# An fp32 sum of 64 features, as two products of 32 features on the column quarters of the PE array

## The chip, the cores and the metric

The kernel runs on one core of a Trainium2 chip. A core has five engines: TensorE (PE, matrix products, with its weight loads shown apart as PEld), VectorE (DVE), ScalarE (ACT), GpSimd (POOL) and SyncE (SP), which issues most DMAs. The metric is the time of one execution on the device in microseconds, the median of several runs. The profile is of one further execution; its span is from the first to the last instruction.

## What is computed

Four graph layers over 3,327 nodes with 64 features, all with the same dense-stored adjacency matrix `adj` (3,327 x 3,327, fp32). Each begins with a layer norm and a ReLU and adds to `x`. What costs time is the product with `adj`, or with a matrix made of it, eight times in a row:

```python
# layer 0: two gated cells            (k = 0, 1)
m = adj @ (h @ W);  ... sigmoid, tanh ...
# layer 1: ranked neighbours          (k = 2)
mask = (adj != 0);  rank = cumsum(mask, axis=1)
w = mask * where(pos > 0, 0.5 ** (k - pos), 0)
out = w @ (h @ weight) + bias
# layer 2: squared weights            (k = 3, 4, 5)
w = adj * adj
for W, b in ((W0, b0), (W1, b1), (W2, b2)):
    x = (w @ x) @ W.T + b
# layer 3: two hops                   (k = 6, 7)
agg = adj @ x;  x = tanh(concatenate([agg, x], 1) @ W[k])
```

## The kernel before

**Tiling.** The nodes are padded to 3,328 and cut into two halves of 13 blocks of 128. The host lays `adj` out transposed. A source block (`Tile`, number `q`, 26 of them) brings 128 source nodes on the partitions and, for each half `h` of the targets, a range of target columns. The 13 target blocks of a half are cut into four chunks, `CH`, of 384, 384, 384 and 512 columns, held in two groups (`GROUPS`). The last sum cuts its second chunk once more, into 256 and 128 columns (`PARTS`).

**A step.** `propagate(k, c, t, ...)` (L579) adds source block `t` to sum `k` of chunk `c`. The stationary operand is the 128 x 64 block of features `yq` of the source nodes, the moving one the 128 x w block of `adj`. It does so once for each target half: half 0 writes to PSUM partitions 0 to 63 of the chunk's accumulator, half 1 to partitions 64 to 127. So the first product sits on the left 64 columns of the PE array, the second on the right 64. These are L605 to L608:

```python
for n, yq in enumerate(terms):
    for h in range(2):
        nc.tensor.matmul(acc[h][1][h * D:(h + 1) * D, :w], yq[h], rhs[h], ...)
```

In seven of the eight sums (`KIND` is PLAIN or SQUARED) both operands are fp32 and there is one term. In the ranked sum (`KIND[2]` is RANKED) both are bf16 and there are three terms a step. 7 sums x 26 sources x 4 chunks, and 26 more for the last sum's extra part, make 754 fp32 steps.

**What stands between the steps.** One order of PE instructions is made when the program is built. `joint` (L655) and `alone` list the steps: sum k of a group of chunks, with steps of sum k + 1 put in between once their sources are known. `run` walks the list. It puts in:
- `count` (L533, products on L542, bf16, 64 columns for each half): the number of non-zero entries of each target column, four products for a source block. They come after nearly every pair of steps of the sums k = 0 and 1.
- `expand` (L484): for the ranked sum the mask is multiplied by a triangular matrix `tri` (through `mm`, L307, bf16, 64 columns), and ACT (L523) or DVE (L521) turns the ranks into powers of two.
- after a chunk's last step, a task `after_k`: copies out of PSUM (L824 on ACT, L825 on DVE), the gates (L876), transposes and small weight products on PE (L307, L774, L791), layer norm (L834 to L849), which makes the features of the next sum.

A task is advanced by `spend`, which takes an estimate of PE time for each step. The order of every engine is thereby fixed at build time; semaphores only hold an instruction back. All products of the kernel before use column tiles of 64.

**Buffers.** 20 slots of SBUF hold source blocks; SP loads them (L405) up to 44 steps ahead. PSUM has eight banks, four for sums and four for temporaries.

Of the kernel before, what the change touches and what calls it, by code (L numbers as in the profile page):

```python
# [44 lines left out]
N, D = 3327, 64  # L45
# [25 lines left out]
PLAIN, RANKED, SQUARED = range(3)  # L71
KIND = [PLAIN, PLAIN, RANKED, SQUARED, SQUARED, SQUARED, PLAIN, PLAIN]
# [11 lines left out]
def chunk_of(b):  # L84
    return next(c for c, (b0, b1) in enumerate(CH[:NC]) if b0 <= b < b1)
# [11 lines left out]
def kernel(  # L97
# [9 lines left out]
    nc = tc.nc  # L107
# [191 lines left out]
    def width(c):  # L299
        return blocks(c) * P  # L300
# [15 lines left out]
    def take(sums=False, either=True):  # L316


        either = either and not sums
        pool = idle_sums if sums else idle_temps  # L320
        if either and idle_sums and (not pool or released[idle_sums[0]] < released[pool[0]]):
            pool = idle_sums
        for c in list(tasks):
            if not pool and c not in running:
                advance(c)
        i = pool.popleft()
        return i, banks[i]
# [25 lines left out]
    def advance(c):  # L353
        running.add(c)
        try:
            tasks[c][1] = next(tasks[c][0])
        except StopIteration:
            del tasks[c]
        running.discard(c)

    def begin(c, task):
        finish(c)
        tasks[c] = [task, 0.0]
        advance(c)

    def finish(c):
        while c in tasks:
            advance(c)
# [5 lines left out]
    def spend(us):  # L374

        for c in list(tasks):
            if c in tasks and c not in running:
                tasks[c][1] -= us
                if tasks[c][1] <= 0:
                    advance(c)  # L380
# [79 lines left out]
    def make_mask(t, kind):  # L460

        t.mask = Mask(t.w)
        rows = P - 1 if kind == RANKED else P

        def piece(half):
            nc.vector.tensor_scalar(t.mask.view[:rows, half], t.view()[:rows, half], 0.0, None, op0=ALU.not_equal)  # L466
            if half == 0 and kind == RANKED:

                for ch in GROUPS[t.g]:
                    finish(("count", ch))  # L470
                nc.gpsimd.dma_start(out=t.mask.view[P - 1:P], in_=totals[t.g][t.q:t.q + D + 1:D, :])  # L471
            if half == 1:
                t.used()

        pieces.extend([(t, 0, piece), (t, 1, piece)])
# [57 lines left out]
    def count(t, first, last):  # L533


        mask_pieces(t=t)
        for c in GROUPS[t.g]:
            w = width(c)
            if first:
                counts[c] = take(either=False)  # L540
            for s in range(2):
                nc.tensor.matmul(counts[c][1][s * D:(s + 1) * D, :w], behind[:, NQ - 1 - t.q:NQ - 1 - t.q + D],  # L542
                                 t.mask.view[:, s, t.cols(c)], start=first, stop=last)
            spend(STREAM_US * w / CWM * 0.25)
            if last:
                begin(("count", c), count_done(c))
        t.mask.free()
# [31 lines left out]
    def propagate(k, c, t, rhs, first, last):  # L579
        if k == COUNT:  # L580
            count(t, first, last)
            return
        w = width(c)
        if first:
            sums[k, c] = [take(sums=True) for _ in range(2 if k == 7 and c == PARTS[1] else 1)]
            sums[k, c] = [sums[k, c][0], sums[k, c][-1]]
        acc = sums[k, c]
        if t is SPECIAL:
            for ch in range(NC):
                while y[k][ch] is None:  # L590
                    advance(ch)
            terms = [[lasty[:, h, i, :] for h in range(2)] for i in range(3)]
            rhs = [rhs, rhs]
        else:
            s, b = divmod(t.q, NB)
            cs = chunk_of(b)
            if y[k][cs] is None:
                finish(cs)
            terms = [[yk[:, b - CH[cs][0], s, :]] * 2 for yk in (y[k][cs] if KIND[k] == RANKED else [y[k][cs]])]
            rhs = [rhs[:, h, :] for h in range(2)]  # L600
            if KIND[k] != RANKED:
                t.used()
            if (k, c, t) in squared:
                squared.pop((k, c, t)).free()
        for n, yq in enumerate(terms):  # L605
            for h in range(2):
                nc.tensor.matmul(acc[h][1][h * D:(h + 1) * D, :w], yq[h], rhs[h], start=first and n == 0,  # L607
                                 stop=last and n == len(terms) - 1)  # L608
        if t is not SPECIAL and t.early and t.mask is None:
            make_mask(t, RANKED)  # L610
        spend(STREAM_US * w / CWM * (0.75 if KIND[k] == RANKED else 1.0))
        if last:
            begin(c, after[k](c, sums.pop((k, c))))
# [97 lines left out]
    def run():  # L711
# [5 lines left out]
        for i, (k, c, t) in enumerate(units):  # L717
# [24 lines left out]
            elif all(y[2][ch] is not None for ch in GROUPS[0]):  # L742
                relief["pieces"] = t is not SPECIAL
                if i % 2 == 0:
                    mask_pieces(1)
            n = done[k, c] = done.get((k, c), 0) + 1
            propagate(k, c, t, expanded.popleft(), n == 1, n == total[k, c])


# [336 lines left out]
```

## Time and profile before

| | us |
|---|---|
| median of 3 runs | 706.8 (706.53 to 707.41) |
| span of the profiled execution | 703.7 |
| DVE and ACT busy | 350.1 and 271.8 |
| longest single wait of PE after the start | 0.9 |
| DMA: mean rate over the span | 286 GB/s |

The profiled execution's span is 3.1 us less than the median of the runs, which include what lies around the instructions.

How to read the views. "Busy" of an engine is the time in which at least one of its instructions is under way. A matmul's end is modelled and includes the time that the pipeline takes to empty, so a busy PE may still have room; what counts is the distance between the starts of passes. In a group, "128*64" is rows times columns of the PE array, "128x384" the moving operand; "xN" the number of instructions, then the busy time, the mean duration in ns, and the idle time ahead of them with what ended it. In the chain of waits each piece has its start and its length in us. The slices are tenths of 40 equal parts of the span.

The waits of PE, longest first in total, with times and longest single wait:

```profile
PE temp L791 <- DVE y L849: 14.9, 1, 14.9
PE sum L307 <- DVE e L521: 1.4, 2, 0.9
PE temp L542 <- DVE adj L466: 0.7, 2, 0.5
PE sum L607 <- DVE y L849: 0.6, 1, 0.6
```

The first is the wait for the first features; the others together are some 4 us.

Busy time of the engines in four stages: to 137 us and from there to 205 us (the first two sums, with their counts between them), to 345 us (the ranked sum beside fp32 sums, from the first instruction of L523 at 204.5 us on), and the rest, nearly all fp32. The numbers in brackets are instructions; the last three columns are the granted clock, the busy share of the DMA engines and GB/s:

```profile
0.00:137.00 137.00, 121.19 (x859) 74.27 (x861) 84.06 (x168) 17.33 (x31) 15.03 (x32) 1.00 0.86 332
137.00:205.00 68.00, 67.78 (x494) 31.99 (x491) 42.59 (x86) 14.61 (x26) 18.05 (x25) 1.00 0.81 291
205.00:345.00 140.00, 136.71 (x1374) 98.90 (x1372) 110.42 (x213) 113.87 (x199) 39.68 (x53) 1.00 0.63 218
345.00:704.00 359.00, 354.11 (x2382) 167.78 (x2378) 113.04 (x282) 125.97 (x169) 7.24 (x5) 1.00 0.78 294
```

### The profile page before, as it was taken

To read this page: it belongs to the slowest core of one execution; us is meant where nothing else is said; L and a number is where in the kernel's file an instruction comes from. 1 tells how busy PE (TensorE), PEld (TensorE's weight loads), DVE (VectorE), ACT (ScalarE), POOL (GpSimd) and SP (SyncE) were. 2 spreads that over 40 slices of the span, in tenths; PEclk is the share of its full clock that TensorE was granted. 3 is DMA by queue.
4 is the path that set the end of the run, shared out by engine and by line. 5 is a ranking of instruction groups with operands and counts; after the bars stand their busy time and mean duration, and the time that the engine had idled before them with its cause. 6 is when DMAs were issued, how large, how long until landed. Compare 5 with 4: busy or idle time off the path is not lost.

```text
span 703.7 us, 12628 instructions
## 1 busy us (share of the span) xinstructions
PE 679.8 (97%) x5100; PEld 372.9 (53%) x5100; DVE 350.1 (50%) x746; ACT 271.8 (39%) x422; POOL 80.0 (11%) x114
## 2 busy tenths in 40 slices
PE   1999999999999999999999999999999999999997
PEld 1454666643556787677444444333344444344586
DVE  7556835643997889847523105425271565005101
ACT  1014100122146888888998206832166600000101
POOL 4300000002284233111100000000000000000000
PEclk9999999999999999999999999999999999999999
DMA  9999996089686952683799649973998399927991
GB/s 344 401 385 404 406 405 241 2 314 398 209 279 253 371 177 76 246 297 96 265 390 343 245 151 409 405 276 100 398 366 271 107 391 406 406 81 276 402 403 45
DMA packets 68549, 201.31 MB, mean 286 GB/s; under 512 B 7228, under 2 KB 8228, under 8 KB 68492
## 3 DMA queue, kind: packets, MB, share of 16 engines
q1 hardware_dynamic: 65596, 199.46, 75.9%
q8 instruction: 40, 0.66, 0.4%
q10 hardware_dynamic: 720, 0.85, 0.3%
q0 software_dynamic: 2176, 0.20, 0.2%
q14 instruction: 17, 0.14, 0.1%
HBM read 199.45 MB, written 0.85 MB: 285 GB/s over the span
## 4 chain that ended last, share of the span: by engine, by line
PE 91%; DVE 7%; issue 0%; ACT 0%; DMA 0%; POOL 0%; ACTq 0%; DVEq 0%; POOLq 0%
PE sum L607 77%; PE temp L307 5%; PE temp L542 2%; PE temp L876 2%; PE sum L307 1%; DVE adj L466 1%; PE temp L774 1%; PE sum L876 1%; DVE e L521 1%; DVE st L842 1%; DVE adj L901 1%; DVE t L836 1%; DVE y L841 0%; DVE st L834 0%; DMA xs<-in_x 0%
## 5 line engine op out<-in xcount | busy, mean ns | idle before, releaser
L607 PE MATMUL sum<-adj,y 128*64 128x384 f32 (+3 forms) x3016 | 534.5, 502 | 0.7 <-DVE y L849 0.6
L607 PEld LDWEIGHTS sum<-adj,y 128*64 128x64 f32 x3016 | 243.5, 137 | 237.3 <-issue 212.4
L440 ACT ACTIVATE adj<-adj 128x768 f32<-128x768 f32 (+1 forms) x176 | 144.2, 893 | 45.8 <-PE sum L607 21.9
L466 DVE TENSOR_SCALAR adj<-adj 128x768 bf16<-128x768 f32 (+3 forms) x208 | 114.0, 597 | 39.8 <-PE temp L542 31.8
L824 ACT COPY both<-sum 64x384 f32<-64x384 f32 (+3 forms) x17 | 8.1, 478 | 192.6 <-PE sum L607 191.4
L607 PE MATMUL sum<-e,both 128*64 128x384 bf16 (+1 forms) x624 | 78.5, 339 | 0.5 <-DVE e L521 0.5
L523 ACT ACTIVATE e<-temp,bitsb 128x384 int16<-128x384 f32 (+1 forms) x117 | 66.0, 605 | 15.1 <-PE temp L307 9.9
L825 DVE COPY both<-sum 64x384 f32<-64x384 f32 (+3 forms) x17 | 9.6, 569 | 110.5 <-ACT both L824 110.5
L307 PE MATMUL temp<-adj,tri 128*64 128x384 bf16 (+1 forms) x332 | 56.8, 341 | 0.5 <-DVE e L521 0.2
L442 DVE TENSOR_TENSOR adj<-adj 128x768 f32<-128x768 f32 (+1 forms) x32 | 30.6, 1005 | 52.1 <-DMA adj<-in_adjT 33.4
L845 POOL TENSOR_TENSOR st<-st,mhalf 128x6 f32<-128x6 f32 (+1 forms) x16 | 24.0, 1498 | 283.2 <-DVE st L843 279.5
L607 PEld LDWEIGHTS <-both 128*64 128x64 bf16 x624 | 46.6, 110 | 15.5 <-issue 2.2
L307 PEld LDWEIGHTS <-tri 128*64 128x64 bf16 x416 | 33.5, 110 | 15.3 <-issue 7.1
L521 DVE TENSOR_SCALAR e<-temp 128x384 int16<-128x384 f32 (+1 forms) x49 | 30.1, 617 | 21.1 <-ACT e L523 10.5
L471 POOL DMA_DIRECT2D adj<-totals x52 | 31.5, 607 | 51.2 <-PE temp L307 40.9
L803 DVE STREAM_TRANSPOSE both<-y 32x96 f32<-32x96 f32 (+1 forms) x128 | 35.6, 278 | 2.9
L542 PE MATMUL temp<-adj,behind 128*64 128x384 bf16 x208 | 30.3, 339 | 0.9 <-DVE adj L466 0.7
L819 DVE STREAM_TRANSPOSE y<-t 32x96 f32<-32x96 f32 (+1 forms) x64 | 17.8, 278 | 24.9 <-ACT t L810 24.0
L542 PEld LDWEIGHTS <-behind 128*64 128x64 bf16 x208 | 17.0, 110 | 17.6 <-issue 15.9
L755 DVE COPY t<-sum 128x384 f32<-128x384 f32 x6 | 3.3, 555 | 35.3 <-PE sum L607 35.3
L564 POOL MEMSET adj<- 128x768 f32 (+1 forms) x2 | 1.9, 950 | 145.3 <-PE sum L607 145.3
L523 ACT ACTIVATE e<-sum,bitsb 128x384 int16<-128x384 f32 (+1 forms) x28 | 16.6, 598 | 2.5 <-PE sum L307 2.1
(132 smaller groups left out, 327.8 us busy)
## 6 DMA issues: line engine op xcount, KB each, us to landing
adj<-in_adjT SPq DMA_DIRECT2D x130, 768.0 KB, 8.5
adj<-in_adjT SPq DMA_DIRECT2D x104, 896.0 KB, 12.3
xs<-in_x SPq DMA_DIRECT2D x1, 640.0 KB
adj<-totals POOLq DMA_DIRECT2D x26, 3.0 KB, 5.1
adj<-totals POOLq DMA_DIRECT2D x26, 3.5 KB, 3.0
out<-xs ACTq DMA_DIRECT2D x2, 192.0 KB
out<-xs ACTq DMA_DIRECT2D x1, 256.0 KB
stage<-in_weights SPq DMA_DIRECT2D x2, 112.0 KB, 13.1
```

Of the source, the lines that this page charges most:

```text
L307: nc.tensor.matmul(out[hs], lhsT[:, hs], rhs, start=start, stop=stop)
L440: nc.scalar.activation(sq, v, AF.Square)
L442: nc.vector.tensor_tensor(sq, v, v, ALU.mult)
L466: nc.vector.tensor_scalar(t.mask.view[:rows, half], t.view()[:rows, half], 0.0, None, op0=ALU.not_equal)
L471: nc.gpsimd.dma_start(out=t.mask.view[P - 1:P], in_=totals[t.g][t.q:t.q + D + 1:D, :])
L521: nc.vector.tensor_scalar(wide[:, s], ps[:, :w], BITS, 0.0, op0=ALU.add, op1=ALU.max)
L523: nc.scalar.activation(wide[:, s], ps[:, :w], AF.Relu, bias=bitsb)
L542: nc.tensor.matmul(counts[c][1][s * D:(s + 1) * D, :w], behind[:, NQ - 1 - t.q:NQ - 1 - t.q + D], t.mask.view[:, s, t.cols(c)], start=firs ...
L607: nc.tensor.matmul(acc[h][1][h * D:(h + 1) * D, :w], yq[h], rhs[h], start=first and n == 0, stop=last and n == len(terms) - 1)
L803: nc.vector.transpose(to[at:at + 32, :, q], h[q * 32:(q + 1) * 32, :, s, f * 32:(f + 1) * 32])
L845: nc.gpsimd.tensor_tensor(st[:, 3, :n], st[:, 2, :n], mhalf[:, :n], ALU.pow)
L876: nc.tensor.matmul(ps[upper(1 - s), :w], cells[:, cell, s, g, :], both[c][:, s], start=True, stop=True)
```

## The change

Every fp32 step now issues four products instead of two. The 64 features of the stationary operand are cut into two runs of 32. For each run `f` and each target half `h`, a product of 32 columns is put at PSUM partitions h x 64 + f x 32, with its place in the array given as `tile_position=(0, at)`: the array works as four column tiles of 32. The moving operand of a half is read by two products, f = 0 and f = 1. The order is quarter 0, 64, 32, 96. The steps of the ranked sum, the counts, the masks' products and all small products stay as they were, on two column tiles of 64.

```diff
-        for n, yq in enumerate(terms):
-            for h in range(2):
-                nc.tensor.matmul(acc[h][1][h * D:(h + 1) * D, :w], yq[h], rhs[h], start=first and n == 0,
-                                 stop=last and n == len(terms) - 1)
+        if KIND[k] != RANKED:
+            for f in range(2):
+                for h in range(2):
+                    at = h * D + f * 32
+                    nc.tensor.matmul(acc[h][1][at:at + 32, :w], terms[0][h][:, f * 32:(f + 1) * 32], rhs[h],
+                                     start=first, stop=last, tile_position=(0, at))
+        else:
+            for n, yq in enumerate(terms):
+                for h in range(2):
+                    nc.tensor.matmul(acc[h][1][h * D:(h + 1) * D, :w], yq[h], rhs[h], start=first and n == 0,
+                                     stop=last and n == len(terms) - 1)
```

Line numbers after this place are seven higher in the changed kernel; the fp32 products are its L609, the ranked ones L614. Nothing else is changed: the estimates that `spend` takes, the list of steps and the order of the other engines are the same.

## The prediction

> **What bounds the kernel now.** I read the page's engine shares and slices first, then the chain of waits, then the groups of PE by shape, then single stretches in the timeline.
>
> The page, its span, engine shares, slices, chain and two groups:
>
> ```profile
> span 703.7 us, 12628 instructions
> PE 679.8 (97%) x5100; PEld 372.9 (53%) x5100; DVE 350.1 (50%) x746; ACT 271.8 (39%) x422; POOL 80.0 (11%) x114
> ...
> PE   1999999999999999999999999999999999999997
> ...
> PEclk9999999999999999999999999999999999999999
> ...
> PE 91%; DVE 7%; issue 0%; ACT 0%; DMA 0%; POOL 0%; ACTq 0%; DVEq 0%; POOLq 0%
> ...
> L607 PE MATMUL sum<-adj,y 128*64 128x384 f32 (+3 forms) x3016 | 534.5, 502 | 0.7 <-DVE y L849 0.6
> L607 PEld LDWEIGHTS sum<-adj,y 128*64 128x64 f32 x3016 | 243.5, 137 | 237.3 <-issue 212.4
> ```
>
> PE is busy from 15 us to the end at the full granted clock, and the changed line is 534.5 us of it, with 0.7 us of idle time before it. The fp32 products of L607 are 1,508 in the program (754 steps of one source block and one chunk, two halves each), yet 3,016 stand in the profile: an fp32 product runs as two passes, each with its own weight load.
>
> How full is the array? The chain of waits has long stretches that hold nothing else:
>
> ```profile
> 365.98 41.28 PE sum L607 x256
> ...
> 413.73 90.87 PE sum L607 x504
> ```
>
> The first is all 384 columns wide: 41.28 us / 256 = 161 ns a pass. A step has four passes, so 645 ns, although one pass lasts 486 ns in the trace. So the two halves stream beside each other, each pass taking 322.5 ns of its half. By the clock that the Trainium skill gives (2.4 GHz; TensorE: Matmul & The Clock Gate, its table of specifications) 384 columns x 4 cycles are 640 ns. The measured 645 leaves 5 ns a step, about 4 us over 754 steps: the columns are all in use, and there is nothing for quarters to fill in such a stretch. Over the whole kernel, 7 sums x 26 sources x 1,664 columns = 302,848 columns of each half, at 645/384 = 1.68 ns, make 509 us.
>
> Two more facts from the timeline and the groups by shape:
>
> ```profile
> 68.51 0.76 PE L876 MATMUL temp<-both,cells 128*64 128x384 f32 x2
> 68.84 0.49 PE L542 MATMUL temp<-adj,behind 128*64 128x384 bf16 x2
> 69.11 0.49 PE L876 MATMUL temp<-both,cells 128*64 128x384 f32 x1
> 69.16 0.60 PE L542 MATMUL temp<-adj,behind 128*64 128x384 bf16 x2
> ```
>
> In the program all passes of this L876 gate stand ahead of the L542 counts, yet two counts start before the last gate pass. The halves take their work independently: the upper half runs ahead while the lower one is still behind. The second fact is the price of a fresh start, from the groups by shape in 341.2 to 341.5 us (after a wait) and in 420.0 to 420.3 us (in a full stream):
>
> ```profile
> L607 PE MATMUL sum<-adj,y 128*64 128x384 f32 x2 | 0.5, 537 | 0.6 <-DVE y L849 0.6
> ```
> ```profile
> L607 PE MATMUL sum<-adj,y 128*64 128x384 f32 x4 | 0.8, 486 | 0.0
> ```
>
> A pass whose weights were not loaded ahead lasts 51 ns more (537 against 486). And 486 against 322.5 says that 164 ns of a pass are the pipeline emptying behind it, hidden as long as the next pass follows.
>
> **What the Trainium skill says.** TensorEngine Tiling (Array Packing), Key Properties: "Mode switching requires drain: Changing tiling mode (not just tile) drains the TensorE". Before has only 64-column tiles, so its trace shows no switch and neither confirms nor denies it. The same section says that tiles operate independently; the timeline above agrees. TensorE: Matmul & The Clock Gate, Part 3, Measured speedup, gives 2.38 times for three column tiles of 32, so quarters do run beside each other; no run here shows a quarter. The same part has matmuls in strict FIFO; the lines at 68.8 us contradict that across halves, and the measurement decides.
>
> **The change part by part.**
>
> Removed and added: every fp32 step (L607, kinds other than RANKED) had two products of 64 columns and gets four of 32, so 1,508 products become 3,016, and 3,016 passes become 6,032, each as wide as before (128 to 512 columns of the moving operand). No instruction of DVE, ACT, POOL or SP is added or moved; the order of these engines and of the DMAs is the same. All bf16 products (L307, L542, the ranked L607) and the small fp32 ones (L774, L791, L876) keep 64-column tiles.
>
> Streaming: a quarter takes two passes of 322.5 ns a step, as a half did. If the four run together a step stays at 645 ns and costs 0 more. What hides the doubled passes is the quarters running side by side. If that cover goes, and only two passes run at a time as in before, a step takes 1,290 ns: +509 us. Both ends are kept. I take 0, because halves demonstrably take their work independently. The order is q0, q64, q32, q96, each with two passes, so the second pass of a quarter has to be overtaken by the first of the next; at 68.8 us such overtaking happens.
>
> Issue and weight loads: eight load-and-pass pairs in 645 ns are one per 81 ns. L774 sustains 208 passes in 8.1 us, one per 39 ns, so issue is no limit at 384. Only at 128 columns in the last sum (26 steps, some 215 ns each, 27 ns a pair) is it near: 26 x 8 x 12 ns = 2.5 us at most, mixed among wider ones; I take 0. A weight load of 32 columns is under its pass (137 ns for 64 against 322.5 ns): 0.
>
> Switches: in the changed program's PE order the tile width changes 196 times, 98 times into quarters and 98 out. By the times of the same places before, 99 lie before 137 us (a COUNT, L542, after almost every pair of steps of the first sums), 24 up to 205 us, 42 up to 345 us (ranked steps between fp32 ones), 31 after. Before, such a change of line costs nothing: L542 has 0.9 us of idle time in all. Price of a drain, from before: 164 ns of emptying pipeline plus a weight load that could not go ahead, 51 ns for 64 columns and by half the columns an estimated 26 for 32. Out of quarters 215, into quarters 190: 98 x 0.215 + 98 x 0.190 = 39.7 us. Lower bound 0 (the quarters are only waited for one by one). Upper bound 0.25 us each, 49 us. I take the price of the drain, because the skill states one. From 205 to 345 us PE is partly held up by the masks (ACT 114 and DVE 110 us busy of 140), and I let half of 42 x 0.2 us, 4 us, vanish there. Elsewhere nothing covers it: PE waits there for almost nothing, its longest wait after the start being 0.9 us.
>
> What is queued behind: everything that waits for a sum (L824, L825 and the tasks after them) comes later by the same amount; the DMAs, 75.9% busy, and the other engines only gain room.
>
> Sum: 39.7 - 4 = 36; 703.7 + 36 = 740 us of span. Before's median is 706.8, 3.1 above its span, so 743.
>
> **Rivals.**
>
> B, switches cost little or nothing (0 to 50 ns): 707 to 717, at 50 ns 196 x 0.05 = 10 us. For it: the halves' independence; a quarter need only wait for its own half. Against it: the skill's sentence.
>
> C, drains as above, and quarters overtake each other only by one waiting pass. A long stretch still fills all four, but a short one of one or two steps starts and ends with two of four at work: one pass more for each of 98 stretches, 416 columns on average, 0.34 us: +33, so 776 (760 to 800). For it: 61 of the 98 stretches hold one or two steps. Against it: the counts at 68.8 to 69.2 us run several ahead.
>
> D, the quarters don't stream at full rate, because reads for four moving operands or weight loads share something. Three of four at once: 509 / 3 = +170, 877; two of four: +509, 1,216, or about 1,250 with the drains. For it: before never reads more than two moving operands at once. Against it: the 2.38 times of the skill for three.
>
> E, the other side, faster: the finer pieces close holes. PE's passes by shape, at two cycles a column for fp32 and one for bf16, two passes at a time, sum to 662 us; from 14.9 to 703.7 us there are 689, so 27 us are an array not full, mostly where one half has run out and the other goes on. Its place is the ends of stretches, as in the lines at 68.8 us. If quarters take up a tenth of it, 2.7 us, the time is 704; this decides only if a switch costs under 2.7 / 196 = 14 ns. Against it: a half could take the next work just as early.
>
> **How the numbers follow.** A change within 0.2% (1.4 us) can't be told from none here. A, full rate with drains: 0.50, 743, by its bounds 725 to 760. B: 0.15, of which 0.05 within 0.2%. C: 0.14. D: 0.18, of which 0.11 above 880. E: 0.03. The predicted time is A's, 743. The range 710 to 880 leaves out E, the part of B within 0.2% and the upper part of D: 0.19. Faster 0.03, same 0.05, slower 0.92.
>
> **What would show it.** Streaming: in the all-fp32 stretch (366 to 407 us before) 512 passes in the same 41 us, PE's mean pass still 486 ns; at 82 us, D. Switches: new idle time of about 0.2 us of streaming at each change between the fp32 steps and L542 or L307, with the first 137 us longer by about 20 us, 137 to 205 by 5, 205 to 345 by 4 to 8, and the rest by 6. C: short stretches longer than their passes by another 0.3 us, long ones not. The prediction is wrong if the long stretches change their pace, or if the first 137 us grow by less than 5 us.

## The result, and the profile after

| | before | changed |
|---|---|---|
| median of 4 runs, us | 706.66 | 729.0 (728.76 to 729.78) |
| span of the profiled execution, us | 703.7 | 727.0 |
| PE matmul passes / fp32 step passes | 5,100 / 3,016 | 8,116 / 6,032 |

The ratio is 1.0316, 95% interval 1.0304 to 1.0329: 22.3 us slower. The spans differ by 23.3 us: the changed kernel's median is 2.0 us above its span, that of before 3.0, so the profiled execution of before was, by estimate, about 1 us faster than its median execution. The page of the changed kernel, in the order of the lines shown of before:

```profile
span 727.0 us, 18660 instructions
...
PE 704.1 (97%) x8116; PEld 299.2 (41%) x8116; DVE 351.0 (48%) x746; ACT 272.1 (37%) x422; POOL 75.8 (10%) x114
...
L609 PE MATMUL sum<-adj,y 128*32 128x384 f32 (+2 forms) x6032 | 530.6, 503 | 0.5 <-DVE y L856 0.3
L609 PEld LDWEIGHTS sum<-adj,y 128*32 128x32 f32 x6032 | 185.2, 110 | 300.5 <-issue 282.0
```

By the shares on this page nothing has happened: PE has the same 97%, the same digit in every slice, a mean pass of 503 ns instead of 502, and even less idle time ahead of the changed line. The chain of waits says more. The long fp32 stretch that began at 365.98 us before is now (start, length, what):

```profile
385.54 41.42 PE sum L609 x512
```

These are twice the passes in 41.42 us instead of 41.28; the other long stretch takes 91.01 instead of 90.87. Four quarters run as fast as two halves did. But the stretch begins 19.6 us later. The time was lost ahead of it. The chain between 95 and 108 us, where two steps' pairs and the counts alternate, first before, then after:

```profile
96.00 3.01 PE sum L607 x16
99.00 0.38 PE temp L542 x4
99.38 3.01 PE sum L607 x16
```
```profile
100.19 3.14 PE sum L609 x32
103.34 0.50 PE temp L542 x4
103.84 3.14 PE sum L609 x32
```

A period of one stretch of fp32 steps and four counts takes 3.38 us before and 3.65 after, from start to start. It holds two changes of tile width, one from quarters to halves and one back, so 0.13 us each. The counts were not edited, and yet their piece grew from 0.38 to 0.50.

What happens at a change is seen in the timeline of PE (start, length, then the group), here around the counts at 107 us, and in the groups by shape, from 106.85 to 107.05 us:

```profile
105.94 1.04 PE L609 MATMUL sum<-adj,y 128*32 128x512 f32 x8
106.91 0.57 PE L542 MATMUL temp<-adj,behind 128*64 128x384 bf16 x4
107.41 0.53 PE L609 MATMUL sum<-adj,y 128*32 128x384 f32 x4
```
```profile
L542 PE MATMUL temp<-adj,behind 128*64 128x384 bf16 x2 | 0.4, 351 | 0.0
```

The eight passes of 512 columns are two for each quarter. How long they stream, that is, take in columns of the moving operand, follows from the distance between two passes of a quarter: 322.5 ns at 384 columns and 429 at 512, so 0.83 ns a column. Two passes of 512 columns stream for 2 x 426 ns, and the last quarter starts some 20 ns after the first: the array has taken in its last column at 106.81. The first count starts at 106.91. For 0.1 us no column enters the array. Then the count's pass takes 351 ns instead of 326, because its weights were not loaded ahead. The weight loads begin at 106.91 too:

```profile
106.91 0.14 PEld L542 LDWEIGHTS <-behind 128*64 128x64 bf16 x4 [0.84 <-issue]
```

The profile shows no idle time of PE, because the modelled end of the last fp32 pass (105.94 + 1.04 = 106.98) lies after the start of the count. In the starts of all passes of the changed kernel, the pause without a column is 93 to 99 ns at 192 of the 196 changes, in both directions and for both types (the four longer ones have a wait in them). The exposed load, the time by which the first pass is longer than others of its shape, is 24 to 26 ns in most, and 51 for an fp32 load of 64 columns.

The growth by stage is read from the starts of the same fp32 steps in the two traces: 135.56, 204.12 and 345.81 us before, 147.69, 218.66 and 364.92 after.

| stage before, us | changes of width | growth, us | per change, us | predicted, us |
|---|---|---|---|---|
| 0 to 137 | 99 | 12.1 | 0.12 | about 20 |
| 137 to 205 | 24 | 2.4 | 0.10 | 5 |
| 205 to 345 | 42 | 4.6 | 0.11 | 4 to 8 |
| 345 to the end | 31 | 4.2 | 0.14 | 6 |

### The profile page after: what moved, and what is told of

Read it like the earlier page. It is cut to its first block, busy times and chain, and to the rows that moved or that the text cites. A ratio compares the mean times of both kernels' runs of the same rounds, so it can differ in the third digit from the quotient of the medians.

```text
span 727.0 us, 18660 instructions
## 1 busy us (share of the span) xinstructions
PE 704.1 (97%) x8116; PEld 299.2 (41%) x8116; DVE 351.0 (48%) x746; ACT 272.1 (37%) x422; POOL 75.8 (10%) x114
## 4 chain that ended last, share of the span: by engine, by line
PE 92%; DVE 6%; issue 0%; DMA 0%; ACT 0%; POOL 0%; ACTq 0%; DVEq 0%; POOLq 0%
PE sum L609 70%; PE sum L614 7%; PE temp L307 6%; PE temp L542 3%; PE temp L883 2%; PE sum L307 1%; PE temp L781 1%; DVE adj L466 1%; PE sum L883 1%; DVE e L521 1%; DVE st L849 1%; DVE adj L908 0%; DVE t L843 0%; DVE y L848 0%; DVE st L841 0%
## 5 line engine op out<-in xcount | busy, mean ns | idle before, releaser
L609 PE MATMUL sum<-adj,y 128*32 128x384 f32 (+2 forms) x6032 | 530.6, 503 | 0.5 <-DVE y L856 0.3
L609 PEld LDWEIGHTS sum<-adj,y 128*32 128x32 f32 x6032 | 185.2, 110 | 300.5 <-issue 282.0
L614 PE MATMUL sum<-e,both 128*64 128x384 bf16 (+1 forms) x624 | 73.0, 340 | 0.5 <-DVE e L521 0.5
L523 ACT ACTIVATE e<-temp,bitsb 128x384 int16<-128x384 f32 (+1 forms) x117 | 66.0, 605 | 19.6 <-PE temp L307 13.1
L307 PE MATMUL temp<-adj,tri 128*64 128x384 bf16 (+1 forms) x332 | 49.6, 343 | 0.5 <-DVE e L521 0.2
L614 PEld LDWEIGHTS <-both 128*64 128x64 bf16 x624 | 39.2, 110 | 21.9 <-issue 8.6
L471 POOL DMA_DIRECT2D adj<-totals x52 | 33.0, 637 | 55.6 <-PE temp L307 46.2
L307 PEld LDWEIGHTS <-tri 128*64 128x64 bf16 x416 | 26.5, 109 | 21.0 <-issue 13.4
L542 PE MATMUL temp<-adj,behind 128*64 128x384 bf16 x208 | 28.6, 348 | 0.4 <-DVE adj L466 0.2
L542 PEld LDWEIGHTS <-behind 128*64 128x64 bf16 x208 | 9.1, 109 | 30.5 <-issue 28.9
```

What stands on the lines that cost most here:

```text
L307: nc.tensor.matmul(out[hs], lhsT[:, hs], rhs, start=start, stop=stop)
L523: nc.scalar.activation(wide[:, s], ps[:, :w], AF.Relu, bias=bitsb)
L609: nc.tensor.matmul(acc[h][1][at:at + 32, :w], terms[0][h][:, f * 32:(f + 1) * 32], rhs[h], start=first, stop=last, tile_position=(0, at))
```

## The experiments

**Theories.** T: each change of tile width on PE costs a pause of 95 ns and an exposed weight load, about 0.12 us; the quarters themselves cost nothing. R1: the cost lies in the doubled products, 22.3 us over 1,508 extra ones, 15 ns each. R2 (rival C of the prediction): a short stretch of quarters fills and empties badly. They are told apart by changing the number of changes and of quarter products separately.

| kernel | fp32 steps in quarters | changes of width | time, us | above before, us | per change, us |
|---|---|---|---|---|---|
| all in quarters | 754 | 0 | 707.2 | 0.6 | |
| late sums only | 546 | 62 | 714.4 | 7.8 | 0.126 |
| counts alone | 0 | 96 | 717.89 | 11.2 | 0.117 |
| counts too | 754 | 128 | 720.46 | 13.8 | 0.108 |
| counts in pairs | 754 | 158 | 725.66 | 19.0 | 0.120 |
| changed kernel | 754 | 196 | 729.0 | 22.3 | 0.114 |
| other order in a step | 754 | 196 | 729.33 | 22.7 | 0.116 |
| masks and small products at 128 columns | 0 | 236 | 730.95 | 24.3 | 0.103 |
| every second block | 533 | 376 | 755.01 | 48.4 | 0.129 |

Each row's difference is to the runs of before on the same chip (706.6 or 706.66). Read by the third column the rows lie on one line of 0.10 to 0.13 us a change; by the second column they lie on none.

**1. No change of width left.** Every product that the changed kernel still writes on a half goes through a helper that writes it on two quarters (ten places, of which the one in `mm` is shown):

```diff
+    def quarters(out, h, lhsT, rhs, start=True, stop=True):
+        for f in range(2):
+            q = slice(f * 32, (f + 1) * 32)
+            nc.tensor.matmul(out[q], lhsT[:, q], rhs, start=start, stop=stop, tile_position=(0, h * D + f * 32))
...
-            nc.tensor.matmul(out[hs], lhsT[:, hs], rhs, start=start, stop=stop)
+            quarters(out[hs], h, lhsT[:, hs], rhs, start=start, stop=stop)
```

> Every product of the kernel, bf16 and fp32, is written on 32-column tiles: no change of tile width is left (196 in the changed kernel). Theory T (each change of width costs about 0.12 us, a pause of 95 ns and an exposed weight load of 24 to 51 ns): 196 x 0.12 = 23.5 us come back, time 705 to 709. Rival R1 (the cost lies in the doubled products, 22.3 us over 1,508 extra ones, 15 ns each): 1,678 fp32 and 1,272 bf16 products more, so 740 or above. Rival R2 (short stretches leave quarters empty at both ends): the stretches are gone too, so 706 to 710, as T.

707.2 us, ratio to before 1.0010 (1.0002 to 1.0018), with 10,200 passes where before has 5,100. R1 falls. (By these passes the extra fp32 products are 1,914, not 1,678; R1's forecast only rises by it.) R2 is not separated from T here. The chain has the period of before, 3.38 us, with all pieces in twice the passes (the helper is L154), and the long stretch at its old length:

```profile
95.72 3.01 PE sum L614 x32
98.72 0.38 PE temp L154 x8
```
```profile
367.85 41.28 PE sum L614 x512
```

fp32 and bf16 products still alternate here as in the changed kernel, so a change of type alone costs nothing. The masks' stage, with its bf16 products in double number, is not quite free. There PE stands still three times, 3.9 us in all, with no cause that the profile names ("issue"); before has no such pause. The longest:

```profile
235.55 2.09 issue
```

The fp32 step at 284.46 us before starts 1.9 us later here, though the one at 204.12 starts 0.4 us earlier. What held PE was not tried.

**2. Quarters where little stands between the steps.**

```diff
-        if KIND[k] != RANKED:
+        if k >= 3:
```

> Quarters only in the sums k = 3 to 7, halves in k = 0 and 1: 62 changes of width instead of 196, and 546 of the 754 fp32 steps in quarters. T: 706.7 + 62 x 0.12 to 0.13 = 714 to 715. R1: 546/754 of 22.3 us, so 722.8. R2: between, by the number of short stretches that are left, 709 to 712.

714.4 us, as T said; R1's 722.8 and R2's 709 to 712 are missed. In the first sums, which are halves again, the chain of waits has the period of 3.38 us again (from 95.80 to 99.18), with a piece of 0.38 us for the counts.

**3. More changes with fewer quarters.**

```diff
-        if KIND[k] != RANKED:
+        if KIND[k] != RANKED and not (k >= 4 and t.q % 2):
```

> In the sums k = 4 to 7, where hardly anything stands between the fp32 steps, every second source block is taken in halves again: 376 changes of width instead of 196, and 221 steps fewer in quarters. T: 180 more changes at 95 + (24 + 51)/2 = 133 ns, +24 us, so 752 to 754. R1: 221/754 of 22.3 us less, so 722.5. R2 (no pause, only one pass of fill for each stretch of quarters): up by 90 x 0.35 = 31 us, 760.

755.0 us: 221 steps fewer in quarters, and 26.0 us more than the changed kernel. T said 24; R1 had the sign wrong, R2 was 5 too high. The chain, quarters on L609 and halves on L614:

```profile
564.18 1.44 PE sum L614 x8
565.62 1.43 PE sum L609 x16
```

Two steps of 384 columns take 2 x 645 ns = 1.29 us within a long stretch; here they take 1.43 in quarters and 1.44 in halves. A short stretch of quarters is no worse than one of halves, so R2's fill is not there. The 2 us above T may come from the end of each stretch, where the last product finishes later because it started later: 20 ns after the first with four quarters, 7 with two fp32 halves. For 90 more stretches of each kind that is an estimated 90 x 27 ns = 2.4 us.

**4. Another order of the four products.**

```diff
-            for f in range(2):
-                for h in range(2):
+            for h in range(2):
+                for f in range(2):
```

> The four products of a step in the order 0, 32, 64, 96 instead of 0, 64, 32, 96, nothing else. T: the same 196 changes, 728.5 to 729.5. R2, if quarters of one half wait for each other in order: a short stretch would fill differently, several us either way (722 to 736).

729.33 us against 729.0; this order makes no difference that counts.

**5. The counts in quarters as well**, the other products as in the changed kernel (L542 through the helper of experiment 1).

> The changed kernel with the counts' products (L542) also in quarters: 128 changes of width instead of 196. T: 729.0 - 68 x 0.12 = 720.8, 719.5 to 722. R1 (extra products cost 15 ns each): 208 products more, 732.

720.46 us, within T's range: more products than in the changed kernel, and less time.

**6. The counts alone in quarters**, on the kernel before.

> The kernel before with the counts alone in quarters, all fp32 products in halves as before: 96 changes of width. T: fp32 to quarters 95 + 24 ns, back 95 + 51 ns, so 96 x 0.133 = +12.8, 718 to 720. R1: no fp32 product is doubled, so at most 208 x 15 ns = +3, below 710.

717.89 us, just below T's 718 to 720. No fp32 product is touched, and 96 changes cost 11.2 us, half of what the change under study costs. T took 24 ns for the exposed load of a count; in this trace a bf16 load of 32 columns exposes 10 to 13. The chain has the period of 3.65 us again, from 96.96 to 100.61 (the counts are L154):

```profile
96.96 3.16 PE sum L612 x16
100.12 0.49 PE temp L154 x8
```

**7. The same products, fewer changes.** In the list of steps the counts come two source blocks at a time:

```diff
-            if len(self.waiting) > self.lag:
-                self.next()
+            if len(self.waiting) > self.lag + 1:
+                self.next()
+                self.next()
```

> The changed kernel with the counts put into the list two source blocks at a time: every product as in the changed kernel, but 158 changes of width instead of 196. T: 729.0 - 38 x 0.12 = 724.4, 723 to 726. R1: all products are there, 729.

725.66 us, 3.3 less than the changed kernel for 38 changes fewer (T: 4.6). All products are those of the changed kernel, so R1's 729 is missed.

**8. No quarter anywhere, but another width.** On the kernel before, `mm`, which makes the masks' products and the small weight products, writes one product of 128 columns:

```diff
-        for h in range(2):
-            hs = slice(h * D, (h + 1) * D)
-            nc.tensor.matmul(out[hs], lhsT[:, hs], rhs, start=start, stop=stop)
+        nc.tensor.matmul(out, lhsT, rhs, start=start, stop=stop)
```

> The kernel before with the helper mm (L302, masks and small weight products) writing one product of 128 columns instead of two of 64: no quarter anywhere, 236 changes between 128 and 64 columns, 118 stretches of one to eleven wide products. If the pause belongs to any change of tile width: 236 x 0.12 = 28 us less some 5 that the masks' stage hides, 728 to 736. If it belongs to quarters alone: 704 to 708.

730.95 us, with 355 passes fewer on PE than before (4,745 on the page against 5,100). The pause belongs to any change of width tried here, not to quarters. Between a step of the ranked sum in 64-column tiles and the masks' product in one of 128 the timeline shows the same:

```profile
208.68 0.66 PE L605 MATMUL sum<-e,both 128*64 128x384 bf16 x6
209.26 0.50 PE L305 MATMUL temp<-adj,tri 128*128 128x384 bf16 x2
209.69 0.68 PE L605 MATMUL sum<-e,both 128*64 128x384 bf16 x6
```

Two masks' products of 384 columns, which follow each other at 163 ns without a change of width, would give way to the next step after 326 ns; here 430 pass.

None of the versions is faster than before.

## Why the prediction was right

The range (710 to 880) and the direction held, and 729.0 also lies within the bounds of its case A (725 to 760). The forecast was 743, 36 us of growth for the measured 22.3: the mechanism was right, and its price was too high. By its own steps:

- *The array is full, quarters can fill nothing.* Right. The long stretch went from 41.28 to 41.42 us.
- *The four quarters stream together, +0.* Right, and the main risk (rival D, +170 to +509 us) did not come. The mean fp32 pass is 503 ns, 502 before.
- *Issue and weight loads cost 0.* Right, with more room than thought: in the kernel with all in quarters, 416 small passes (L154, `w,both`) are done in 7.9 us, 19 ns a pass, where the prediction reckoned with 39.
- *196 changes of width, each a drain.* Right that each change holds PE up: experiments 1, 3, 6 and 8 show it from four sides. The Trainium skill (TensorEngine Tiling (Array Packing), Key Properties) calls this a drain and gives no price. The runs show a pause and its length; that the array empties in it is not shown.
- *The price of a drain, 0.19 to 0.215 us.* This is the step that failed, by its size. The term of 164 ns was read off the modelled end of a pass (486 less 322.5). The pause measures 95 ns. The exposed load was taken as 51 ns out of quarters and 26 into them; it measures 24 to 26 in most cases and 51 only for fp32 loads of 64 columns. With about 0.12 us for a change instead of 0.203 the sum is 196 x 0.12 = 23.5, against 22.3 measured.
- *4 us vanish in the masks' stage.* Not so: from 205 to 345 us 42 changes cost 4.6 us, 0.11 each, hardly less than elsewhere. That 4.6 lies in the forecast of 4 to 8 is luck, a cover that did not come and a price that was too high.
- *3.1 us from span to median.* About 1 us of it was the chance of one profiled execution, as said above.
- Not explained: the pauses (18.8 us, without the waits that four of them hold), exposed loads (5.8) and later starts of the fourth quarter (98 x 13 ns) add to some 26 us where the span grew by 23.3. About 1 us of the difference is waits of PE for other engines, which sum to 19.0 us before and 18.0 after. Where the rest went was not tried.
- *B* (cheap changes) and *C* (short stretches that fill badly) both fell; *E* (quarters close holes) found no gain: with no change of width left, the kernel is 0.1% slower than before.

## What to carry to other kernels

In this kernel fp32 products split onto narrower column tiles cost nothing by themselves as long as everything around them had the same width, and gained nothing, since the wider tiles already filled the array. The price is in the seams, the places where the width changes. Count them in the order of PE's instructions, at the 0.10 to 0.13 us each that these runs show, and keep one width through a stage, or put the odd products together so that one seam serves several. The busy share of PE does not show a seam; compare the starts and lengths of matching pieces in the chain.

## What the runs showed that was not expected

- The pause is alike for 32, 64 and 128 columns: 93 to 99 ns at most changes, bf16 or fp32, in either direction.
- The exposed load depends on what is loaded. For fp32 it is 24 ns at 32 columns, 51 at 64 and 104 at 128 (the last in the run of experiment 8), for bf16 11 at 32 (experiment 6), 24 at 64 and 11 at 128 (experiment 8).
- The pause is shorter than the tail that the profile models behind a pass (164 ns). Here a pass's modelled end is thus no measure of when products of another width can start.
- Two fp32 passes of a quarter behave as those of a half: 322.5 ns for 384 columns, four at a time, started some 7 ns apart. The weight load of 32 columns is listed with 110 ns, that of 64 with 137; halving the columns saves a fifth of the listed time.
